# Context attentions: a group's negated maxima are sent to a row of its query tile by eight DMAs, in place of transposes and a subtraction

## The chip, the cores and the metric

The kernel runs on one core of a Trainium2 chip. The metric is the device time of one execution in microseconds (us). The kernel before takes 2529.41 us in the median of three runs (2527.76 to 2529.56). Engines are named as in the profile: PE is TensorE's matrix multiplication and PEld its weight load, DVE is VectorE, ACT is ScalarE, POOL is GpSimd, and SP is SyncE, which here only issues DMAs.

## The reference

The program is a decoder of four layers on x of 4 batches x 256 positions x 128 features, in float32. Each layer has a self attention, a cross attention to one context of 4 x 1601 x 96, and a feed-forward part. Each part is followed by a residual sum and a layer norm. The change concerns the cross attentions of the first and the third layer, called the context attentions here:

```python
x = _layernorm(x + _L0_attn_ref(x, ...))
x = _layernorm(x + _L0_xattn_ref(x, ctx_768, ...))     # context attention, 16 heads of 8
x = _layernorm(x + _L0_ffn_ref(x, ...))
x = _layernorm(x + _L1_attn_ref(x, ...))               # 16 heads of 8, queries and keys normalised
x = _layernorm(x + _L1_xattn_ref(x, ctx_768, ...))
x = _layernorm(x + _L1_ffn_ref(x, ...))
x = _layernorm(x + _L2_attn_ref(x, ...))
x = _layernorm(x + _L2_xattn_ref(x, ctx_768, ...))     # context attention, 16 heads of 8
...                                                    # L2 ffn, then L3 attn, xattn, ffn

def _L0_xattn_ref(x, context, context_mask, Wq, Wk, Wv, Wo):
    ...                                  # q: 16 heads x 256 x 8; k, v: 16 heads x 1601 x 8
    scores = jnp.einsum('bhid,bhjd->bhij', q, k) * scale
    attn = jax.nn.softmax(scores, axis=-1)
    out = jnp.einsum('bhij,bhjd->bhid', attn, v)
    out = out.transpose(0, 2, 1, 3).reshape(B, N, DIM)
    return out @ Wo
```

For a softmax whose exponents stay small, the greatest score of every query (over 1601 keys) is taken from its scores before the exponential.

## The kernel before

The program runs in stages, one after the other: a setup, the self attention of L0 (the first layer), a long stage `middle` (64 to 1115 us in the profile), the feed-forward part of L2, the attentions of L3, and the last part. The change lies in `middle`. It holds the context attentions of L0 and L2 and everything between them.

**Groups and parts.** Four heads make a group. Each head has a slot of 32 partitions in a query tile `Q` (128 x 256) and in a key tile `K` (128 x 1601), of which rows 0 to 7 hold the head's features. Row 16 of each slot (`RS`) is the row of the maxima: in `K` it is one, and in `Q` as computed it is zero, so whatever stands in `Q`'s row 16 is added to all the scores of that query. Two layers, four batches, two key tiles and two query tiles for each give 32 groups, numbered 0 to 31 here. A group's 1601 keys are gone through twice, each time in seven parts.

**Two passes.** The first pass, `maxima` (L951-975), multiplies queries by keys (`one<-K,Q`) and reduces each piece to its maximum (L968, into `M`). With the seventh part, a last reduction (L974) puts 128 x 8 maxima (two halves of the queries, four heads) into columns of a zeroed tile `mpad`. One round later, `shift` (L1065) calls `shifted` (L578-586): it transposes the two halves of `mpad` on TensorE by multiplying with the identity. While `self.narrow` holds, `mm` (L416) cuts a product into pieces of 32 columns, so that a transpose is four products; the sixteen matrix instructions that the profile counts for one group are `one<-c,mpad`. DVE then subtracts the result from `Q` (L585), giving the shifted queries `q2`. The second pass, `scores` (L1020), multiplies keys by `q2`, ACT takes the exponential (L1002, `E`), and `sums` (L1028) multiplies by the values (`one<-E,V`). ACT copies the product (L1045, `part`, two buffers) and POOL adds it to the group's sum (L1046, `acc_sb`).

**The loop.** One pass of the loop from L1125 on is a round, `p`. A round issues the maxima of one part and the scores of another, interleaved by pairs of heads (`jp`: the scores take heads 2 and 3 first), then the sums of the part whose scores were made in the round before. The first pass is up to nine parts ahead of the second. The scores of a group may begin two rounds after its shift, which is three rounds after its last maxima: `shifted_at` (L1148).

**What is woven in.** `life(b)` (L1089) is a generator that each round moves one step on, for each batch: it does the output of L0's context attention, L0's feed-forward part, and the layer L1 up to L2's self attention. Its self attentions hand 24 blocks of four heads, `Own`, to the same loop (16 in L1's attention, 8 in `l1_masked`). An own block first gathers its queries and keys with four DMAs from SBUF to SBUF on SP's queue (L1132; `QK<-w` and `w<-w` in the profile), and keeps the transposes (`own_shift`). In L1's attention (`l1_queries`), POOL raises norms to a power in eight pieces `rn` (L1346), one step of the generator each. `l1_xattn` loads a tile `rows` for each batch (L1381), and `life` of the last batch loads four packs of weights for later stages, `up`, `gp`, `down` and `p3_0` (L1110-1111, by `load`, L371). All of these loads go by SP's queue.

**The order.** `manual_schedule(engines=...)` (L1124) keeps PE, DVE and ACT in the order of the source. POOL's and SP's instructions are placed by the scheduler of the framework, which can move them against the source. A DMA signals its end through one of eight completion semaphores, taken in turn; the next DMA that is given the same semaphore waits for the one before it.

Of the kernel before, what the change touches and what calls it, by code (L numbers as in the profile page):

```python
# [17 lines left out]
ALU = mybir.AluOpType  # L18
AX = mybir.AxisListType
# [3 lines left out]
P = 128  # L23
NB = T // P
# [20 lines left out]
SW = 32  # L45
VS = 17
VW = 2 * 16 * VS + 16
RS, RX = 16, 17
# [14 lines left out]
class Own:  # L63
    pad = q2 = None
# [254 lines left out]
class Net:  # L319
# [48 lines left out]
    def misc(self):  # L368
        return self.tile("one", [P, 512], pool=self.ps_one)

    def load(self, name, keep=False, parts=(0,), width=None):  # L371
        src = self.dram[name]
        if keep:
            t = self.tile(name, [P, src.shape[1]], pool=self.const)
        else:
            t = self.tile(f"w{SLOT[name]}", [P, width or src.shape[1]], pool=self.wpool)
        for lo, hi in zip(parts, parts[1:] + (src.shape[1],)):
            self.nc.sync.dma_start(t[:, lo:hi], src[:, lo:hi])
        self.packs[name] = t

    def loaded(self, name):
# [467 lines left out]
    def middle(self):  # L849
# [7 lines left out]
        nc = self.nc  # L857
# [22 lines left out]
        for i in range(3):  # L880
            t = self.tile(f"V{i}", [P, NCH * 4 * VS + 16], bufs=1)
# [5 lines left out]
        for i in range(5):  # L887
            if i:
                t = self.tile(f"QK{i}", [P, 2, T], bufs=1)
            else:  # L890
                t = self.spot["QK"].rearrange("p (k t) -> p k t", t=T)
# [10 lines left out]
        pairs = [(s, b, kt) for s in range(2) for b in range(B) for kt in range(2)]  # L902
        n_groups = 2 * len(pairs)
        n_parts = 7 * n_groups
        ks, qs, ms, q2s, accs, es, outs = {}, {}, {}, {}, {}, {}, {}
        later, fresh = [], {0: set(range(B)), 1: set()}
        left = {(s, b): 4 for s in range(2) for b in range(B)}

# [42 lines left out]
        def maxima(i, p, jp):  # L951
            if p == 0 and jp == 0:
                ms[i] = self.tile("M", [P, NB, 4, 4], bufs=3)
            heads = [(j, self.misc()) for j in range(2 * jp, 2 * jp + 2)]
            at = 0
            for n, lo, hi in PARTS[p]:
                for j, ps in heads:
                    r = slice(SW * j, SW * j + KR)
                    self.mm(
                        ps[:, at : at + hi - lo], qs[i][r, n * P : (n + 1) * P],  # L960
                        ks[i // 2][r, lo:hi],
                    )
                at += hi - lo
            for j, ps in heads:
                at = 0
                for n, lo, hi in PARTS[p]:
                    part = p - 3 * n
                    nc.vector.reduce_max(  # L968
                        out=ms[i][:, n, j, part : part + 1], in_=ps[:, at : at + hi - lo], axis=AX.X
                    )  # L970
                    at += hi - lo
            if p == 6 and jp == 1:
                pad, at = self.next_mpad()
                nc.vector.reduce_max(out=at, in_=ms.pop(i), axis=AX.X)  # L974
                ms[i] = pad

        def own_maxima(u, jp):
            if jp == 0:
# [41 lines left out]
        def scores(m, jp):  # L1020
            if isinstance(m, Own):
                score(m.t[:, 1, :], m.q2, P, range(NB), jp, m, m.scale)
                return
            i, k = divmod(m, 7)
            cs, kp = chunks(k)
            score(ks[i // 2], q2s[i], kp, cs, jp, m, scale)

        def sums(m):  # L1028
            if isinstance(m, Own):
# [29 lines left out]
        def own_ended(u, sb):  # L1059
# [1 line left out]
            out = outs[u.b][:, :, 4 * u.hd * u.g : 4 * u.hd * (u.g + 1)]  # L1061
            self.collected(sb, out.rearrange("p n (j d) -> p n j d", d=u.hd), u.hd)
            u.count[0] -= 1

        def shift(i):  # L1065
            q2s[i] = self.shifted(qs[i], ms.pop(i), bufs=2)

        def own_shift(u):
            u.q2 = self.shifted(u.t[:, 0, :], u.pad, "Q2s", 2)
# [19 lines left out]
        def life(b):  # L1089
            while left[0, b]:  # L1090
                yield
            yield
            yield from self.l0_output(b, outs.pop(b))
            yield from self.l0_ffn(b)
            qk = yield from self.l1_queries(b)
            yield from attend(b, qk, "qa", 4, 8, 1.0)
            yield
            y = self.y(b)
            nc.vector.tensor_add(y, self.x[b], outs.pop(b))
            yield from self.block_end_steps(b, y)  # L1100
            y = yield from self.l1_xattn(b)
            yield from self.block_end_steps(b, y)
            qk = yield from self.l1_masked(b)
            yield from attend(b, qk, "raw", 2, 16, D**-0.5)
            yield
            yield from self.l1_output(b, outs.pop(b))
            yield from self.l2_attn(b)
            fresh[1].add(b)
            if len(fresh[1]) == B:
                for n in ("up", "gp", "down", "p3_0"):  # L1110
                    self.load(n)
            while left[1, b]:
                yield
            yield CUT if b == B - 1 else None
            yield from self.l2_output(b, outs.pop(b))
            self.gates[b] = yield from self.l2_gate(b)

        self.gates = {}
        lives = [life(b) for b in range(B)]
        engines = {nc.tensor.engine, nc.vector.engine, nc.scalar.engine}  # L1120
        self.narrow = True
        to_shift, shifted_at = {}, {}
        at_m, at_s, last, p, prepared = 0, 0, None, 0, 0
        with self.tc.manual_schedule(engines=engines):  # L1124
            while at_s < n_parts or last is not None or later or line or lives:  # L1125
                for u in [u for u in line if free[u.hd]][:1]:
                    line.remove(u)
                    u.t = free[u.hd].pop(0)
                    for j in range(4):
                        o = (4 * u.g + j) * u.hd  # L1130
                        src = u.qk.rearrange("p (k t) -> p k t", t=T)
                        nc.sync.dma_start(  # L1132
                            u.t[SW * j : SW * j + u.hd, :, :], src[o : o + u.hd, :, :]
                        )
                    u.ready = p + 1
                    under_way.append(u)
                    if u.last:
                        self.drop(u.dense)
                m = s = None
                for u in under_way:  # L1140
                    if m is None and u.pad is None and u.ready <= p:
                        m = u
                    if s is None and u.q2 is not None and u.turn <= p:
                        s = u
                if m is None and at_m < n_parts and at_m - at_s <= 9:
                    if at_m % 14 or prepared > at_m // 14:
                        m = at_m
                if s is None and at_s < n_parts and shifted_at.get(at_s // 7, p) + 2 <= p:  # L1148
                    s = at_s
                own_m = isinstance(m, Own)  # L1150
                ctx_m = not own_m and m is not None
                if own_m:
                    own_maxima(m, 0)
                elif ctx_m:
                    maxima(*divmod(m, 7), 0)
                if s is not None:
                    scores(s, 1)
                    scores(s, 0)
                if own_m:
                    own_maxima(m, 1)  # L1160
                elif ctx_m:
                    maxima(*divmod(m, 7), 1)
                if last is not None:
                    sums(last)
                for f, *args in to_shift.pop(p, ()):
                    f(*args)
                if own_m:
                    to_shift.setdefault(p + 1, []).append((own_shift, m))
                    m.turn = p + 3
                elif m is not None:  # L1170
                    for f, *args in other.pop(m, ()):
                        f(*args)
                    at_m += 1
                    if m % 7 == 6:
                        to_shift.setdefault(p + 1, []).append((shift, m // 7))
                        shifted_at[m // 7] = p + 1
                if first and first[0][0] <= at_m:
                    f, *args = first[0][1:]
                    (st, b, _), part = pairs[args[0]], args[-1]
                    if f is keys or b in fresh[st]:  # L1180
                        f(*args)
                        first.pop(0)
                        if f is keys and part == 2:
                            prepared = args[0] + 1
                if isinstance(s, Own):
                    under_way.remove(s)
                    free[s.hd].append(s.t)
                elif s is not None:
                    at_s += 1
                last = s  # L1190
                self.advance(later)
                self.advance(lives)
                p += 1
# [174 lines left out]
    def l1_xattn(self, b):  # L1368
# [9 lines left out]
        nc.vector.tensor_scalar_add(q, ps[:, :T], self.w("p1", "xqb"))  # L1378
        rows = self.tile("rows", [P, NCH, CR], bufs=1)
        at = slice(b * NCH * CR, (b + 1) * NCH * CR)  # L1380
        nc.sync.dma_start(rows.rearrange("p c d -> p (c d)"), self.dram["ctx_rows"][:, at])  # L1381
        ends = [(lo, min(lo + 512, S2)) for lo in range(0, S2, 512)]
        yield
        ps = self.misc()
# [728 lines left out]
```

## Time and profile before

| | |
|---|---|
| median of three runs | 2529.41 us |
| the profiled execution | 2529.01 us |
| its span, first to last instruction | 2526.8 us |
| mean granted TensorE clock | 0.986 |
| stage `middle` | 64 to 1115 us |
| busy in `middle` (1051 us): PE, DVE, ACT, POOL | 1013.0, 754.1, 694.7, 222.3 us |
| DMA share in `middle` | 0.04 of 16 engines |
| L968, reductions of the first pass, DVE | 1024 of 565 ns |
| L1002, exponentials of the second pass, ACT | 992 of 575 ns |
| L1046, sums on POOL | 192 of 730 ns |

The profile's rows have this form: a line of the kernel, an engine, an operation, the tile written and the tiles read (buffer numbers left out), shapes, and the number of instructions. A row of the timeline begins with its start and its length in us; brackets hold the idle time before it and what ended that. The rows for stretches of time hold, after the length, the busy time of each engine with its number of instructions, then the granted clock (1.00 is full speed), the DMA engines' busy share, and GB/s. "SPq" is SP's queue of instructions, where a DMA's row is its issue: smallest, median and largest duration in ns, then first and last start in us.

### The profile page before, as it was taken

The page shows a single profiled execution, that of the slowest core. Times are in us where ns is not written, and L with a number is a line of the kernel's source. Part 1 is how long each engine was busy: PE and PEld are TensorE (multiplying, and loading weights), DVE is VectorE, ACT ScalarE, POOL GpSimd, SP SyncE. Part 2 cuts the span into 40 slices and gives each one's busy share as a digit, 9 for nine tenths or more (in the row PEclk, how much of TensorE's full clock was granted, in tenths as well). Part 3 has the DMA queues.
Part 4 walks back from the last instruction along what each step waited for, and adds up shares of the span by engine and source line. Part 5 has one row for each costly group of instructions (what it writes and reads, how often), then busy time and mean ns, then how long its engine had stood idle before and what let it go on. Part 6 is the DMA issues. An engine that isn't in the chain of part 4 may idle for free.

```text
span 2526.8 us, 88631 instructions
## 1 busy us (share of the span) xinstructions
PE 2413.9 (96%) x38941; PEld 1668.2 (66%) x38941; DVE 1740.3 (69%) x3802; ACT 1566.3 (62%) x3123; POOL 320.4 (13%) x414
## 2 busy tenths in 40 slices
PE   7999999999999999999999999989899999999997
PEld 4565657666666665668877777766566666666665
DVE  6776766757777777745556666657767776877875
ACT  2676666665666666665535555556666676776674
POOL 3113131131311212110011111011000000000000
PEclk9999999999999999999999999999999999999998
DMA  4000000000000012000030000000000000000000
GB/s 132 2 2 2 7 2 17 7 14 10 2 22 3 2 33 81 2 2 1 1 106 13 26 13 12 12 6 2 2 2 2 5 2 2 5 3 2 5 2 4
DMA packets 14929, 36.19 MB, mean 14 GB/s; under 512 B 4040, under 2 KB 7372, under 8 KB 13648
## 3 DMA queue, kind: packets, MB, share of 16 engines
q1 hardware_dynamic: 14544, 30.53, 4.3%
q8 instruction: 306, 5.01, 0.8%
q14 instruction: 79, 0.65, 0.1%
HBM read 23.67 MB, written 0.52 MB: 10 GB/s over the span
## 4 chain that ended last, share of the span: by engine, by line
PE 83%; DVE 9%; ACT 2%; POOL 2%; issue 2%; POOLq 0%; DVEq 0%; ACTq 0%
PE one L421 68%; PE big L421 14%; DVE M L968 3%; PE one L428 2%; POOL rn L1346 1%; DVE St L1954 1%; DVE ln_st L519 1%; DVE mpad L988 0%; DVE w L1920 0%; ACT E L670 0%; DVE rec L2002 0%; ACT St L1961 0%; DVE ln_mv L521 0%; DVE m L1397 0%; DVE x L530 0%
## 5 line engine op out<-in xcount | busy, mean ns | idle before, releaser
L968 DVE TENSOR_REDUCE M<-one 128x1 f32<-128x458 f32 (+3 forms) x1024 | 513.1, 565 | 160.7 <-PE one L421 160.2
L1002 ACT ACTIVATE E<-one 128x512 f32<-128x512 f32 (+1 forms) x992 | 484.5, 575 | 187.4 <-PE one L421 186.6
L421 PE MATMUL one<-K,Q 32*128 32x458 f32 (+3 forms) x2048 | 435.0, 527 | 3.6 <-ACT part L1045 3.2
L421 PE MATMUL one<-Q,K 32*128 32x256 f32 (+1 forms) x3328 | 396.7, 391 | 0.0
L1910 ACT COPY St<-big 128x1024 f32<-128x1024 f32 (+1 forms) x224 | 204.1, 959 | 133.5 <-PE big L421 133.5
L421 PEld LDWEIGHTS one<-Q,K 32*128 32x128 f32 (+1 forms) x3328 | 262.1, 181 | 34.2 <-issue 5.8
L421 PE MATMUL one<-E,V 128*32 128x256 f32 (+1 forms) x3328 | 230.3, 389 | 19.8 <-DVE M L968 18.1
L1954 DVE TENSOR_TENSOR St<-St,Mb 128x1024 f32<-128x1024 f32 (+1 forms) x224 | 245.2, 1140 | 1.8 <-ACT Mb L1948 1.8
L1961 ACT ACTIVATE St<-St 128x1024 f32<-128x1024 f32 (+1 forms) x224 | 215.4, 1014 | 27.3 <-DVE St L1954 27.0
L421 PE MATMUL one<-St,V 128*32 128x256 f32 (+1 forms) x3328 | 223.5, 387 | 7.7 <-ACT xT L510 6.4
L1046 POOL TENSOR_TENSOR acc_sb<-acc_sb,part 128x256 f32<-128x256 f32 x192 | 140.1, 730 | 703.5 <-ACT part L1045 701.5
L421 PEld LDWEIGHTS one<-K,Q 32*128 32x128 f32 x2048 | 176.0, 184 | 80.0 <-issue 26.2
L421 PE MATMUL big<-Q,K 64*128 64x256 f32 (+1 forms) x1664 | 212.6, 390 | 0.0
L525 POOL TENSOR_TENSOR ln_r<-ln_ve,half 128x2 f32<-128x2 f32 x92 | 68.4, 743 | 1092.0 <-DVE ln_ve L523 1086.6
L1920 DVE TENSOR_TENSOR w<-w,St 128x1024 f32<-128x1024 f32 (+1 forms) x160 | 179.2, 1120 | 32.6 <-ACT St L1910 25.0
L631 DVE TENSOR_REDUCE Ms<-one 128x3 f32<-128x384 f32 x256 | 130.2, 550 | 87.7 <-PE one L421 86.6
L421 PEld LDWEIGHTS big<-Q,K 64*128 64x128 f32 (+1 forms) x1664 | 146.6, 182 | 58.8 <-issue 23.9
L421 PEld LDWEIGHTS one<-E,V 128*32 128x32 f32 (+1 forms) x3328 | 87.0, 109 | 146.7 <-DVE M L968 94.0
L421 PE MATMUL one<-xT,w 128*32 128x256 f32 (+2 forms) x1136 | 164.7, 390 | 4.4 <-DVE M L968 2.5
L421 PEld LDWEIGHTS one<-St,V 128*32 128x32 f32 (+1 forms) x3328 | 113.8, 111 | 70.9 <-ACT xT L510 7.4
L670 ACT ACTIVATE E<-one 128x384 f32<-128x384 f32 x256 | 104.9, 496 | 86.0 <-PE one L421 85.9
L421 PEld LDWEIGHTS big<-w,ctx 96*32 96x32 f32 x3328 | 93.6, 110 | 55.9 <-issue 55.0
(315 smaller groups left out, 4013.8 us busy)
## 6 DMA issues: line engine op xcount, KB each, us to landing
QK<-qk SPq DMA_DIRECT2D x256, 16.0 KB
w<-in_p SPq DMA_DIRECT2D x12, 274.0 KB
rows<-in_ctx_rows SPq DMA_DIRECT2D x4, 630.5 KB
ctx<-in_ctx SPq DMA_DIRECT2D x4, 600.4 KB
w<-in_down SPq DMA_DIRECT2D x1, 2112.0 KB
w<-in_up SPq DMA_DIRECT2D x1, 1632.0 KB
w<-in_gp SPq DMA_DIRECT2D x1, 1632.0 KB
w<-in_p SPq DMA_DIRECT2D x4, 384.0 KB
```

Of the source, the lines that this page charges most:

```text
L421: self.nc.tensor.matmul(out[at], lhsT[:, at], rhs, start=start, stop=stop)
L428: self.nc.tensor.transpose(out, in_, self.ident)
L525: nc.gpsimd.tensor_tensor(rstd, ve, self.half[:, :NB], ALU.pow)
L631: nc.vector.reduce_max(out=m[:, j, :], in_=ps[:, : 3 * P].rearrange("p (s c) -> p s c", c=P), axis=AX.X,)
L670: nc.scalar.activation(es[t, j], ps[:, :w], AF.Exp, scale=scale)
L968: nc.vector.reduce_max(out=ms[i][:, n, j, part : part + 1], in_=ps[:, at : at + hi - lo], axis=AX.X)
L1002: nc.scalar.activation(e[:kp, :w], ps[:kp, :w], AF.Exp, scale=scale)
L1046: nc.gpsimd.tensor_add(accs[i], accs[i], part)
L1910: nc.scalar.copy(st[:kp, :, :nc_, :], ps[:kp, :, :nc_, :])
L1920: nc.vector.tensor_max(to, to, sts[u, k][:kp, :, :nc_, :])
L1954: nc.vector.tensor_sub(e, e, top[u][:kp].unsqueeze(2).broadcast_to([kp, 2, nc_, T]))
L1961: nc.scalar.activation(e, e, AF.Exp, scale=HD**-0.5)
```

## The change

The last reduction of a group now writes a small tile `negm` (128 x 2 x 4, three buffers) with the negated maxima. Eight DMAs on SP's queue, one for each half of the queries and each head, each carry one column of 128 numbers, one from each partition, into half of one row 16 of the query tile itself. The transposes, the subtraction and the tiles `q2s` are gone, and the second pass reads `Q`. The scores of a group may begin three rounds after its last maxima, as before (`turn`). Own blocks keep `own_shift`. The loads of `up`, `gp`, `down`, `p3_0` and of `rows` are issued by ACT in place of SP. POOL's and SP's instructions are now kept in the order of the source too.

```diff
-    def load(self, name, keep=False, parts=(0,), width=None):
+    def load(self, name, keep=False, parts=(0,), width=None, queue=None):
...
-            self.nc.sync.dma_start(t[:, lo:hi], src[:, lo:hi])
+            (queue or self.nc.sync).dma_start(t[:, lo:hi], src[:, lo:hi])
...
             if p == 6 and jp == 1:
-                pad, at = self.next_mpad()
-                nc.vector.reduce_max(out=at, in_=ms.pop(i), axis=AX.X)
-                ms[i] = pad
+                neg = self.tile("negm", [P, NB, 4], bufs=3)
+                nc.vector.tensor_reduce(neg, ms.pop(i), AX.X, ALU.max, negate=True)
+                for n in range(NB):
+                    for j in range(4):
+                        at = SW * j + RS
+                        nc.sync.dma_start(
+                            qs[i][at : at + 1, n * P : (n + 1) * P], neg[:, n, j : j + 1]
+                        )
...
-            score(ks[i // 2], q2s[i], kp, cs, jp, m, scale)
+            score(ks[i // 2], qs[i], kp, cs, jp, m, scale)
...
-        def shift(i):
-            q2s[i] = self.shifted(qs[i], ms.pop(i), bufs=2)
...
                 for n in ("up", "gp", "down", "p3_0"):
-                    self.load(n)
+                    self.load(n, queue=nc.scalar)
...
         engines = {nc.tensor.engine, nc.vector.engine, nc.scalar.engine}
+        engines |= {nc.gpsimd.engine, nc.sync.engine}
...
-                if s is None and at_s < n_parts and shifted_at.get(at_s // 7, p) + 2 <= p:
+                if s is None and at_s < n_parts and turn.get(at_s // 7, p + 1) <= p:
...
                     if m % 7 == 6:
-                        to_shift.setdefault(p + 1, []).append((shift, m // 7))
-                        shifted_at[m // 7] = p + 1
+                        turn[m // 7] = p + 3
...
-        nc.sync.dma_start(rows.rearrange("p c d -> p (c d)"), self.dram["ctx_rows"][:, at])
+        nc.scalar.dma_start(rows.rearrange("p c d -> p (c d)"), self.dram["ctx_rows"][:, at])
```

More of the change, by code (lines that the diff above doesn't have):

```diff
@@ L904, in middle @@
         n_parts = 7 * n_groups
-        ks, qs, ms, q2s, accs, es, outs = {}, {}, {}, {}, {}, {}, {}
+        ks, qs, ms, accs, es, outs = {}, {}, {}, {}, {}, {}
         later, fresh = [], {0: set(range(B)), 1: set()}
@@ L1120, in middle @@
         engines = {nc.tensor.engine, nc.vector.engine, nc.scalar.engine}
+        engines |= {nc.gpsimd.engine, nc.sync.engine}
         self.narrow = True
-        to_shift, shifted_at = {}, {}
+        to_shift, turn = {}, {}
         at_m, at_s, last, p, prepared = 0, 0, None, 0, 0
```

## The prediction

> **What bounds the kernel now.** I read the engine rows and the chain on the page first, then the busy time by stretches, the timeline around one group's end, and last the waits and the DMA issue rows.
>
> ```profile
> PE 2413.9 (96%) x38941; PEld 1668.2 (66%) x38941; DVE 1740.3 (69%) x3802; ACT 1566.3 (62%) x3123; POOL 320.4 (13%) x414
> ...
> PE 83%; DVE 9%; ACT 2%; POOL 2%; issue 2%; POOLq 0%; DVEq 0%; ACTq 0%
> ```
>
> TensorE is busy 96% of the span and holds 83% of the chain that ended last. So work taken from it counts, and a new wait of it counts in full. The change sits in the stage `middle`, 64 to 1115 us, where the columns are length, then busy PE, PEld, DVE, ACT, POOL, the granted clock, DMA.
>
> ```profile
> 150.00:250.00 100.00, 94.10 (x1430) 57.88 (x1422) 70.07 (x163) 64.05 (x148) 30.20 (x32) 0.95 0.01 2
> ...
> 750.00:850.00 100.00, 98.98 (x1921) 68.64 (x1924) 72.19 (x178) 67.76 (x156) 16.56 (x23) 1.00 0.02 5
> ```
>
> The undisturbed stretch leaves TensorE 1 us idle in 100. The other shows an exception: 6 us idle, clock 0.95. The timeline says what that is:
>
> ```profile
> 230.52 12.85 POOL L1346 TENSOR_TENSOR rn<-ss,half 128x8 f32<-128x8 f32 x8
> ...
> 235.52 0.59 PEld L421 LDWEIGHTS one<-E,V 128*32 128x32 f32 x16 [0.35 <-DVE M L968]
> ...
> 236.52 0.19 PEld L421 LDWEIGHTS one<-K,Q 32*128 32x128 f32 x2 [0.41 <-DVE M L968]
> ...
> 237.02 0.19 DVE L974 TENSOR_REDUCE mpad<-M 128x8 f32<-128x32 f32 x1
> ...
> 238.38 0.59 PEld L421 LDWEIGHTS one<-E,V 128*32 128x32 f32 x16 [0.35 <-DVE M L968]
> ...
> 239.05 0.56 PEld L421 LDWEIGHTS one<-c,mpad 128*32 128x32 f32 x16
> ...
> 239.81 0.19 PEld L421 LDWEIGHTS one<-K,Q 32*128 32x128 f32 x2 [0.20 <-issue]
> ...
> 239.95 0.42 DVE L585 TENSOR_TENSOR Q<-Q,one 128x256 f32<-128x256 f32 x1
> ...
> 244.09 0.37 ACT L1045 COPY part<-one 128x256 f32<-128x256 f32 x1 [4.25 <-POOL acc_sb L1046]
> ...
> 244.51 1.90 PE L421 MATMUL one<-K,Q 32*128 32x458 f32 x4 [3.23 <-ACT part L1045]
> ```
>
> A round of the loop is 2.9 to 3.6 us (weight loads of K,Q at 236.52 and 239.81). The eight `rn` powers, one per round in the source, were drawn together into one run of 12.85 us; `acc_sb` adds wait behind it, then ACT, then TensorE, which afterwards runs at clock 0.50 for 6.8 us. Two short stretches, in the same columns as above, show that, and a stall of 2.51 us at 638 that left the clock alone:
>
> ```profile
> 243.20:249.90 6.70, 5.39 (x36) 2.35 (x40) 1.17 (x2) 2.18 (x7) 3.03 (x5) 0.50 0.01 2
> 638.30:645.00 6.70, 4.20 (x80) 2.83 (x80) 6.67 (x19) 2.89 (x8) 0.69 (x1) 1.00 0.01 2
> ```
>
> **The change, part by part.** The sum is against the profiled execution: 2529.01 us, span 2526.8 with 2.2 around it, 0.4 below the median of 2529.41. The built order of the instructions shows TensorE, DVE and ACT otherwise unchanged.
>
> 1. *Transposes gone.* Per group, from the weight load of E,V to that of the next K,Q: 239.81 - 238.38 = 1.43 with the shift, 236.52 - 235.52 = 1.00 without; medians over all such rounds 1.438 and 1.001. So 0.437 x 32 groups = **-14.0 us**, on the path.
>
> 2. *Subtraction gone:* 32 x 0.42 = 13.4 us of DVE, which is busy 72% and waits for TensorE in these rounds: 0 (bounds 0 to -2). The negated reduction replaces one of 188 ns: 0.
>
> 3. *GpSimd in source order.* Each `rn` (1.64 us) now alternates with an `acc_sb` add (0.73): 2.4 us in a round of 2.9 or more, so the run and its stall go; every add is at most 1.6 us later, which the two `part` buffers cover. Three of the four runs cost idle TensorE: 3.23 (here), 4.24 (at 359) and 6.08 (at 525), together 13.55, each followed by clock 0.50 (17.0 us of it outside the gaps; 8.5 us if all were TensorE's). I take 60% of that, 5.1, since the round from 244.51 to 248.96 took 4.45 instead of about 3.4. **-18.6** (bounds -13.5 to -22). The fourth run delayed nothing.
>
> 4. *The new way of the maxima.* After L974, SP issues eight transfers of 128 x 1, then the scores start: the first pair of heads needs the seventh and eighth. The scores' place is unchanged, three rounds on. The time from the end of L974 to the scores' first matmul, group by group, is 2.55 us for the first group, 3.65 for the last, 4.30, 5.38, 5.76, 5.76, 5.87, 6.14, 6.15, 6.49, 6.74, 7.17, 7.57 and above for the rest. Each loses the 0.44 of point 1; group 7 (of 0 to 31; 11.77) loses its 5 us stall too, to 6.3.
>
> What must fit there: wake 0.05 (SP rows start 0.03 to 0.06 after their releaser), seven issue pitches, one transfer, 0.05 for TensorE. No row has 4-byte pieces. The nearest rows:
>
> ```profile
> L1132 SPq DMA_DIRECT2D QK<-w x80: 523/624/1099, 268.3 to 894.3; - x80
> L1132 SPq DMA_DIRECT2D w<-w x16: 507/577/647, 462.4 to 891.2; - x16
> L1381 SPq DMA_DIRECT2D rows<-in_ctx_rows x4: 322/328/348, 38.6 to 711.9; - x4
> ```
>
> Issues between two places in SBUF take 0.58 to 0.62, those from HBM 0.33 to 0.43 whatever their pieces (4 to 256). The new ones are SBUF to SBUF: 0.60, plus 0.045 between issues and 0.047 for a second semaphore wait (both seen at L1132, pitch 0.717 with and 0.668 without): pitch 0.69. Landing: 1.95 to 1.97 after the issue starts, by the semaphore events of L1132 and L1817. L = 0.05 + 4.83 + 1.97 + 0.05 = 6.9. Lateness by group: 4.8, 3.7, 3.0, 2.0, 1.6, 1.6, 1.5, 1.2, 0.85, 0.6, 0.6, 0.2 = **+21.7** (without group 27, next point). Bounds: pitch 0.43 as from HBM gives L 5.1 and 6.3; pitch 0.74 with the longer SBUF landings of the trace (3.2) gives L 8.5 and 47.
>
> The Trainium skill speaks against these transfers: "DMA: Bandwidth & Descriptors", Rules for kernel authors, says that a last dimension that isn't contiguous becomes one descriptor per element and is to be rearranged. No run here shows such a transfer. If each of an engine's eight descriptors took what the trace's 512-byte packets take (27 ns), each landing would be 0.2 us later and this sum 2.4 us larger.
>
> 5. *Loads on ACT's queue.* `up`, `gp`, `down`, `p3_0` are now issued back to back after the ACT copy at 986.46. They hold completion semaphores 0 to 3, and SP's fifth to eighth transfer of group 27 wait for the same four. Singly, 1632 KB landed after 6.4 us and 2112 KB after 8.0: 1.1 + 3.3 per 1000 KB, so 6472 KB land at 987 + 22 = 1009, the eighth transfer at 1011, against scores due at 1003.6 (row at 1004.03): **+7.6** (bounds 0 to 9). The eight issues on ACT, 0.33 each, lie in its idle 38%: 0 to +1, taken as 0. The `rows` loads land in 4.1, long before use.
>
> 6. *SP in source order.* A block's own QK copies now queue behind the eight issues. Group 8's reduction ends at 267.07 and own copies were issued at 268.26 for matmuls at 273.53: pushed to 272.6, last landing 276.7, 3.6 late, of which 0.85 is in point 4: **+2.8** (bounds 0 to 4). Elsewhere at least 0.2 us is left.
>
> 7. *The clock.* In `middle`, gaps of 3.23 and up were followed by 0.50, that of 2.51 at 638 was not. Five stalls of 3 us or more arise (groups 27, 0, 31, 28, own), at 5.1 / 3 = 1.7 each: **+8.5** (bounds 0 to 14). The Trainium skill, "TensorE: Matmul & The Clock Gate", Part 1, halves the clock only after an idle window of about 3.4 us; by that the 3.0 stall goes free, and the sum would be 1.7 lower. The 3.23 row decides for me.
>
> Sum: -14.0 - 18.6 + 21.7 + 7.6 + 2.8 + 8.5 = +8.0, so **2537 us**, 0.3% slower.
>
> **Rivals.** A change under 0.2% (5 us) can hardly be told from none.
> - *Cheap issues, faster.* If an SBUF issue with sixteen engines costs what one from HBM does, pitch 0.43: losses 6.3 + 7.6 + 1 + 3.4 = 18.3, 2529.0 - 32.6 + 18.3 = 2515. For it: out<-x, which reads SBUF, issues in 0.375. Against: every SBUF to SBUF row is 0.51 or more. It decides below a pitch of about 0.60.
> - *Cancelling.* Pitch near 0.6: losses about 32, 2529 within 5 us.
> - *Slow small pieces.* L 8.5: losses 47 + 9 + 5 + 14 = 75, 2571. For it: the piece count, eight transfers in flight at once. Against: the queue moves 2 GB/s here.
>
> **How the numbers follow.** 2537 (2534 to 2552) 0.38; cheap issues 0.27; cancelling 0.20; slow pieces 0.15. Faster 0.27, same 0.20, slower 0.53. The bounds of points 4 and 5 set the range, 2513 to 2567: it takes in the cheap case and most of the slow one.
>
> **What the next profile would show.** Point 1: no `one<-c,mpad` beyond the own ones, 1.0 us from E,V to K,Q. Point 3: no `rn x8`, no TensorE wait on `acc_sb`. Point 4: issues of 0.6, TensorE waits of 1 to 5 us for `Q<-negm` in about twelve groups, the early ones and the last four above all. Point 5: one wait of about 8 us near 1000. Point 7: more half-clock stretches. I am wrong downwards if an issue takes 0.45 or less, upwards if the eighth transfer lands 8 us or more after the reduction.

## The result, and the profile after

The changed kernel takes 2535.27 us in the median of 15 runs (2529.44 to 2541.46), the kernel before 2528.77 in 15 runs beside it (2526.46 to 2533.31). The ratio is 1.0025, with a 95% interval of 1.0017 to 1.0033: 0.25% slower, 6.5 us, against a forecast of 0.3% and 8.0 us. The profiled execution took 2533.71 us (span 2531.9), 4.7 us more than the one before.

The page's engine rows and the chain that ended last, of the changed kernel:

```profile
PE 2419.6 (96%) x38429; PEld 1659.7 (66%) x38429; DVE 1730.1 (68%) x3770; ACT 1567.1 (62%) x3123; POOL 320.4 (13%) x414
...
PE 84%; DVE 9%; ACT 2%; issue 2%; DMA 1%; SPq 0%; POOL 0%; POOLq 0%; DVEq 0%; ACTq 0%
```

TensorE executes 512 matrix instructions fewer and is busy 5.7 us longer. POOL, 2% of the chain before, is down to 0%, and DMA has come in with 1%. The same two stretches of time as before (length, PE, PEld, DVE, ACT, POOL, clock, DMA):

```profile
150.00:250.00 100.00, 97.87 (x1560) 61.92 (x1553) 74.02 (x175) 71.12 (x163) 22.27 (x27) 1.00 0.03 2
750.00:850.00 100.00, 98.98 (x1902) 67.87 (x1900) 71.62 (x177) 67.33 (x156) 16.34 (x23) 1.00 0.05 9
```

Where POOL's run of powers stood, TensorE now does 98 us of work in 100 at full clock (94 at 0.95 before). What came in its place is seen in the timeline at three spots: group 0, an own block behind group 8, and group 27.

```profile
64.99 5.06 SPq L978 DMA_DIRECT2D Q<-negm  x8
...
70.90 2.40 PE L421 MATMUL one<-Q,K 32*128 32x256 f32 x12 [3.80 <-DMA Q<-negm]
...
272.74 5.44 SPq L978 DMA_DIRECT2D Q<-negm  x8
278.28 4.19 SPq L1135 DMA_DIRECT2D QK<-w  x6
...
280.48 1.22 PE L421 MATMUL one<-QK 32*128 32x256 f32 x4 [1.81 <-DMA QK<-w]
...
978.33 0.33 ACTq L378 DMA_DIRECT2D w<-in_up  x1
...
979.67 0.64 ACTq L378 DMA_DIRECT2D w<-in_p  x1
980.41 1.09 ACT L1007 ACTIVATE E<-one 128x512 f32<-128x512 f32 x2 [2.00 <-PE one L421]
...
991.00 8.44 SPq L978 DMA_DIRECT2D Q<-negm  x8
...
1000.09 0.67 PE L421 MATMUL one<-Q,K 32*128 32x256 f32 x2 [2.01 <-DMA Q<-negm]
```

SP needs 5.06 us to issue the eight transfers of group 0, and TensorE stands for 3.80. At 272.74 SP is busy with a group's eight, so the own copies start at 278.28 and TensorE waits for them. At 991 the eight need 8.44, behind loads that ACT issued from 978.33 on. Their four issues also hold ACT itself for 2 us: its exponentials start at 980.41 only. The clock was halved after each of these and after two more waits:

```profile
70.30:80.50 10.20, 9.60 (x72) 6.14 (x72) 3.61 (x9) 3.26 (x6) 0.00 (x0) 0.50 0.01 2
281.90:288.70 6.80, 6.80 (x62) 5.07 (x59) 3.48 (x6) 3.09 (x7) 0.72 (x1) 0.50 0.12 22
1002.10:1008.90 6.80, 6.80 (x49) 3.19 (x48) 2.54 (x5) 3.82 (x9) 0.72 (x1) 0.50 0.00 1
1032.80:1036.30 3.50, 3.50 (x34) 1.30 (x33) 1.49 (x3) 1.70 (x4) 0.00 (x0) 0.51 0.02 5
1107.90:1114.80 6.90, 6.90 (x68) 3.58 (x68) 0.43 (x2) 4.40 (x10) 0.72 (x1) 0.51 0.01 2
```

These are the only stretches in `middle` at half clock. They follow group 0, the own block, and groups 27, 28 and 31. TensorE counts as busy in them because its slower products fill the time. That is one reason why its busy time rose although it has less to do. The other is that many of the waits for the transfers don't show as idle time: idle time that ended with `Q<-negm` comes to 6.9 us at three places, and the pairing below finds losses at eleven groups. At group 1, four `one<-K,Q` products run by themselves from 98.35 to 99.39 us, and the first `one<-Q,K` starts at 99.70, after only 0.31 us of idle time.

DVE executes the same 1024 reductions (L968) in the same order in both kernels, so their starts can be paired one by one. The table gives by how much the difference between the two traces changed at each place:

| place | in the forecast, us | in the traces, us |
|---|---|---|
| each group's border without a wait | -0.44 | -0.43 to -0.45 |
| the three runs of `rn` (243, 359, 525 us) | -18.6 | -6.5, -6.8, -8.7: -21.9 |
| group 0 | 4.8 + 1.7 of clock | +7.1 |
| groups 1 to 4 | 6.7 | +1.5, +1.9, +1.9, +1.3: +6.6 |
| groups 7 and 24 | 1.2 | +2.3, +2.1 |
| own block behind group 8 | 3.6 + 1.7 | +5.7 |
| group 27 | 7.6 + 1.7 | +8.4 |
| groups 28, 30, 31 | 7.9 + 3.4 | +3.3, +0.8, +5.1 |
| other groups | 0.2 | +1.7 |

All that was added comes to some 43 us, all that was removed to 14.0 + 21.9. A half-clock stretch of before at 191.9 us is gone as well (-1.6). The setup, which both have, took 1.1 us longer in this execution, and the stages behind `middle` 2.3 less. Of the 8.4 us at group 27, 1.5 come ahead of its scores, behind ACT's four issues.

### The profile page after: what moved, and what is told of

Its sections match the earlier page's. It is cut to its first block, busy times and chain, and to the rows that moved or that the text cites. A ratio compares the mean times of both kernels' runs of the same rounds, so it can differ in the third digit from the quotient of the medians.

```text
span 2531.9 us, 88233 instructions
## 1 busy us (share of the span) xinstructions
PE 2419.6 (96%) x38429; PEld 1659.7 (66%) x38429; DVE 1730.1 (68%) x3770; ACT 1567.1 (62%) x3123; POOL 320.4 (13%) x414
## 4 chain that ended last, share of the span: by engine, by line
PE 84%; DVE 9%; ACT 2%; issue 2%; DMA 1%; SPq 0%; POOL 0%; POOLq 0%; DVEq 0%; ACTq 0%
PE one L421 68%; PE big L421 14%; DVE M L968 3%; PE one L428 2%; DVE mpad L993 1%; DVE St L1956 1%; DVE ln_st L519 1%; DMA Q<-negm 0%; DVE w L1922 0%; ACT E L670 0%; DVE m L1399 0%; DVE rec L2004 0%; ACT St L1963 0%; DVE x L530 0%; DVE ln_mv L521 0%
## 5 line engine op out<-in xcount | busy, mean ns | idle before, releaser
L968 DVE TENSOR_REDUCE M<-one 128x1 f32<-128x458 f32 (+3 forms) x1024 | 514.5, 566 | 182.0 <-PE one L421 181.5
L421 PE MATMUL one<-K,Q 32*128 32x458 f32 (+3 forms) x2048 | 442.0, 531 | 0.4 <-ACT w L1507 0.4
L421 PE MATMUL one<-Q,K 32*128 32x256 f32 (+1 forms) x3328 | 402.7, 396 | 12.0 <-DMA Q<-negm 6.9
L421 PEld LDWEIGHTS one<-K,Q 32*128 32x128 f32 x2048 | 181.2, 186 | 78.9 <-issue 25.8
L421 PE MATMUL one<-QK 32*128 32x256 f32 (+1 forms) x1344 | 122.4, 374 | 11.1 <-ACT E L670 7.4
```

What stands on the lines that cost most here:

```text
L421: self.nc.tensor.matmul(out[at], lhsT[:, at], rhs, start=start, stop=stop)
L968: nc.vector.reduce_max(out=ms[i][:, n, j, part : part + 1], in_=ps[:, at : at + hi - lo], axis=AX.X)
```

## The experiments

The kernel before ran beside every one of them, at 2528.2 to 2528.6 us in the median.

### What the parts are worth

POOL's order alone, in the kernel before:

```diff
+        engines |= {nc.gpsimd.engine}
```

> The kernel before with one part of the change: POOL in the order of the source. Transposes, subtraction and SP's scheduler stay. My theory (point 3): the three stalls behind the runs of eight rn powers go with their half-clock stretches, 18.6 us (13.5 to 22), so 2510 us (2507 to 2515). The drift between the two traces, which falls by 6.5, 6.8 and 8.7 us at the three places, would say 2507. Rival: the runs of rn cost nothing by themselves, since the rounds behind them catch up or since the stalls only show together with the transposes: 2529 us, as before.

Measured: 2508.21 us, ratio 0.9925 (0.9912 to 0.9939), 20 us less than before. POOL's timeline in this kernel:

```profile
228.82 0.73 POOL L1046 TENSOR_TENSOR acc_sb<-acc_sb,part 128x256 f32<-128x256 f32 x1 [8.25 <-ACT part L1045]
229.68 1.65 POOL L1347 TENSOR_TENSOR rn<-ss,half 128x8 f32<-128x8 f32 x1
232.88 0.73 POOL L1046 TENSOR_TENSOR acc_sb<-acc_sb,part 128x256 f32<-128x256 f32 x1 [1.55 <-ACT part L1045]
```

Powers and adds alternate, POOL idles 1.55 us in the round, and no stretch of `middle` runs at half clock. Paired with the trace before, the gain in `middle` falls at the three places (-6.5, -6.8 and -8.7 us) and at the half-clock stretch of before at 191.9 us, which is gone here too (-1.6). This execution, 2502.24 us, is below the median; some 4 us of its difference lie behind `middle`, which has no part in the change. So this part of the change is a gain by itself and doesn't need the transfers.

The other way round, the changed kernel with POOL left to the scheduler:

```diff
-        engines |= {nc.gpsimd.engine, nc.sync.engine}
+        engines |= {nc.sync.engine}
```

> The changed kernel with POOL left to the scheduler again; SP stays in the order of the source. My theory: the rn powers stand together in runs of eight again and the three stalls come back, 18.6 us (to 22): 2554 to 2557 us. Rival: in the changed kernel the adds have room behind the late scores, so that the runs are hidden: 2535 us.

Measured: 2554.02 us, ratio 1.0105 (1.0091 to 1.0119), 18.8 us above the changed kernel. The run is back in POOL's timeline of this kernel, with the adds queued behind it:

```profile
242.67 12.86 POOL L1348 TENSOR_TENSOR rn<-ss,half 128x8 f32<-128x8 f32 x8
255.49 2.33 POOL L1051 TENSOR_TENSOR acc_sb<-acc_sb,part 128x256 f32<-128x256 f32 x3
```

The late scores didn't hide it. And the changed kernel without its eight transfers:

```diff
-                for n in range(NB):
-                    for j in range(4):
-                        at = SW * j + RS
-                        nc.sync.dma_start(
-                            qs[i][at : at + 1, n * P : (n + 1) * P], neg[:, n, j : j + 1]
-                        )
```

> The changed kernel without the eight DMAs of a group; the maxima are computed but not subtracted. My theory: all that the change costs hangs on these DMAs (points 4 to 7), so what is left is the gain of points 1 and 3, 14.0 + 18.6 = 32.6 us (at most 36): 2493 to 2497 us. No wait on negm, and a half clock only where before had one without POOL. Rival: part of the loss comes from the source order of SP or from the loads on ACT's queue; then the time stays above 2505 us.

Measured: 2500.01 us, ratio 0.9893 (0.9880 to 0.9907). So the transfers cost 35 us in the changed kernel, and all else that it does is worth 28 us of gain. Source order of SP shows no cost without them: the wait at 280 us and the one of group 27 are gone from this trace. The time is still 3 us above the upper end of the expectation, and only 8.2 us below the kernel with POOL's order alone, where 14.0 of transposes separate the two.

Paired with that kernel's trace, this one is only 5.1 us ahead at the end of `middle`. The clock takes most of the rest: this trace has 3.4, 6.8 and 3.4 us at half clock at 52, 69 and 615 us, the other none there, and loses 4.1 us at the first two and 1.5 at the third. Another 1.5 us go behind ACT's four issues for the loads, as in the changed kernel, and 0.9 at 331 us, beside one of the loads of `rows`. So loads on ACT's queue aren't free; no run leaves them on SP's. Of the half clock at 52 and 69 us the cause is open; none of the added transfers stand there. It means that of the 7.1 us at group 0 only some 4 are the transfers': the rest is in this trace too.

### Number, queue and lead of the transfers

Four transfers in place of eight, each with one head's 256 maxima in order (the first pass takes every second query as a block):

```diff
+                neg = self.tile("negm", [P, 4, NB], bufs=3)
...
+                for j in (2, 3, 0, 1):
+                    at = SW * j + RS
+                    nc.sync.dma_start(qs[i][at : at + 1, :], neg[:, j, :])
...
-                        ps[:, at : at + hi - lo], qs[i][r, n * P : (n + 1) * P],
+                        ps[:, at : at + hi - lo],
+                        qs[i][r, :].rearrange("r (p n) -> r n p", n=NB)[:, n, :],
```

> The changed kernel with four DMAs for a group in place of eight: the first pass takes every second query as a block, so that a head's 256 maxima go to one row in order, in pieces of 8 bytes; heads 2 and 3 first. My theory (the lateness is issue pitch times number, then one landing): heads 2 and 3 have landed 0.06 + 0.64 + 1.97 = 2.7 us after the reduction, all four after 4.0, against 5.9 and 6.5. That is late for the first group only (0.7 us); group 27 stays behind the loads, up to 8 us with its clock; own copies wait 2.6 us less. 2528.8 - 14 - 22 + 0.7 + 8 + 1 = 2503 us (2500 to 2510). Rival 1: loading every second query as weights is slower (K,Q weight loads above 184 ns on average); 20 ns more would be some 20 us of weight loads, partly hidden: 2510 to 2523. Rival 2: the lateness doesn't follow the number of DMAs: 2530 or more.

Measured: 2502.74 us, ratio 0.9902 (0.9888 to 0.9916). All four have landed 3.9 us after the reduction in most groups, against 6.5 with eight, and TensorE's idle time that ends with `Q<-negm` is 0.2 us in all, against 6.9. Weight loads of every second query took 191 ns in the mean, 185 in the kernel without transfers; paired with that trace, this kernel loses 0.06 us for a group. (There are 2048 of them, so 20 ns more would have been 41 us and not 20.)

The eight split over two queues:

```diff
-                        nc.sync.dma_start(
+                        (nc.scalar if j in (1, 3) else nc.sync).dma_start(
```

> The changed kernel with the transfers of heads 1 and 3 issued by ACT, those of heads 0 and 2 by SP. My theory (the lateness is the pitch of one queue, 0.64 us, times its transfers): all eight have landed 0.06 + 3 x 0.64 + 1.97 = 4.0 us after the reduction in place of 6.5, late for the first group (1.9 us) and the last (0.8) only. Point 4 falls from about 20 us to 3, point 6 from 5.7 to about 1, point 7 by some 5; group 27 stays behind the loads. That is 26 to 27 us less, 2509 us; against it stand 128 issues on ACT, 70 us in its idle 38%, and ACT's wait for the reduction ahead of its next copy: 0 to 1 us for each group. 2509 to 2535 us, 2515 as the likeliest. Rival: the transfers themselves are slow (eight in flight at once, pieces of 4 bytes), so that two queues land no earlier: 2535 us or more.

Measured: 2589.52 us, ratio 1.0234 (1.0220 to 1.0247), far outside. The first half of the theory held: all eight landed 4.5 us after the reduction in most groups, 2 us earlier, with a pitch of 0.64 on SP's queue and 0.69 on ACT's, and the stall of group 0 was gone. ACT's side I had at 0 to 1 us for a group. Its timeline with TensorE's, and its waits in this kernel (us in total, times, longest):

```profile
89.43 3.74 ACTq L978 DMA_DIRECT2D Q<-negm  x4
93.26 0.37 ACT L1050 COPY part<-one 128x256 f32<-128x256 f32 x1 [4.09 <-PE one L421]
...
93.69 1.39 PE L421 MATMUL one<-K,Q 32*128 32x458 f32 x3 [1.18 <-ACT part L1050]
```

```profile
ACT part L1050 <- DMA Q<-negm: 57.7, 17, 4.4
```

ACT has to pass through the four issues, 2.4 us or more, before its copy of the round's sums, and TensorE waits for the copy. The difference to the changed kernel grows by 1 to 5 us in nearly every group and is 56 us at the end. ACT's idle 38% was no room at that place.

One round more between the passes:

```diff
-                        turn[m // 7] = p + 3
+                        turn[m // 7] = p + 4
...
-                if m is None and at_m < n_parts and at_m - at_s <= 9:
+                if m is None and at_m < n_parts and at_m - at_s <= 10:
```

> The changed kernel with a group's scores one round later (four rounds after its last maxima in place of three) and the first pass up to ten parts ahead in place of nine. My theory: a round of 2.9 us or more covers the lateness of all groups but the first (0.8 us left) and 27 (5 of 8 left). Point 4 goes nearly whole (20 us), point 5 by 3, half of the clock's share (5); point 6 stays. The second pass ends a round later: +1 to 2. 2535.3 - 28 + 2 = 2509 us (2505 to 2516). Rival: the lateness is not what the waits cost, since a round that has only one of the two passes arises at each group's border, with PE waiting for DVE there: 2530 us or more.

Measured: 2509.46 us, ratio 0.9927 (0.9914 to 0.9940). The scores' first products come 8 to 17 us after the reduction in all groups but the first and the last, group 0 waits 1.38 us where it had 3.80, and group 27 doesn't wait. The eight transfers still land at 6.5 to 8.4 us. So for most groups it is the lead that was short by a few us; the rival, a loss through rounds with one pass only, didn't come. The number fits better than its terms: group 27's transfers, at 979 us, now stand 20 us behind the loads (issued from 957.8 on) and don't meet them, so this run doesn't say what a round of lead does there. Point 6's wait, which I had said stays, went at 280 us, but one of 1.69 us for `QK<-w` arose at 417, and the clock was halved at 192.9, 418.2 and 964.3 us.

### The loads and the own copies

The four loads seven rounds later:

```diff
+                for _ in range(7):
+                    yield
                 for n in ("up", "gp", "down", "p3_0"):
                     self.load(n, queue=nc.scalar)
```

> The changed kernel with the loads of up, gp, down and p3_0 seven rounds later, that is behind the eight transfers of group 27. My theory (point 5): the wait of group 27 goes, 8.0 us by the drift between the traces (-8.4 to -0.4 there), so 2527 us (2525 to 2529). The loads have landed some 22 us later, about when group 28's reduction ends; later stages need them 100 us on. Rival 1: the same wait moves to group 28: 2533 us or more. Rival 2: the stall at 998 us is SP's order and not the loads: 2535 us.

Measured: 2529.02 us (2521 to 2538), ratio 1.0002 (0.9989 to 1.0014). Paired with the changed kernel's trace, group 27 gains 5.8 us, and 1.5 more go where the loads were issued before; 1.7 come back where ACT issues them now, and 1.0 at group 28. TensorE's wait there is 2.28 us where it was 1.24, as some of the transfers now land beside the loads (after up to 4.3 us):

```profile
1020.38 1.56 PE L421 MATMUL one<-Q,K 32*128 32x256 f32 x11 [2.28 <-DMA Q<-negm]
```

The rest of the difference lies ahead of that, in the setup and in half-clock stretches of other lengths. The point stands, with a part of the first rival in it. The issues' price only moved.

Own blocks' first pass two rounds behind their copies:

```diff
-                    u.ready = p + 1
+                    u.ready = p + 2
```

> The changed kernel with the maxima of an own block two rounds behind its copies in place of one, so that copies queued behind a group's eight transfers have a round more. My theory (point 6): the wait at 278 us and its half clock go, 5.7 us by the drift between the traces (+5.1 to +10.8 there); elsewhere 24 blocks stand a round later, which costs 0 to 2 us. 2530 us (2528 to 2532). Rival: the copies weren't late by SP's queue but by their source or by the DMA engines; then a round more does it as well, but the issues in the trace start as soon as the copies are due. If the step at 278 us is a matter of group 8's own lateness, the time stays at 2535 us.

Measured: 2546.42 us, ratio 1.0070 (1.0055 to 1.0085), 11 us slower than the changed kernel where 5 faster was expected. The wait at 278 us and its half clock did go. But all that follows stands elsewhere, and near 990 us a new loss arises. ACT's and TensorE's timeline there:

```profile
982.57 0.39 ACTq L378 DMA_DIRECT2D w<-in_gp  x1
988.75 0.33 ACTq L378 DMA_DIRECT2D w<-in_down  x1
994.60 0.34 ACTq L378 DMA_DIRECT2D w<-in_p  x1
995.03 2.06 ACT L1007 ACTIVATE E<-one 128x512 f32<-128x512 f32 x4 [12.72 <-DMA Q<-negm]
...
995.68 1.64 PE L421 MATMUL one<-Q,K 32*128 32x256 f32 x5 [8.51 <-ACT E L1007]
```

The loads now mix with the eight transfers in the turn of completion semaphores: `down` got the semaphore that `up` held, and `p3_0` (`w<-in_p` here) one that a small transfer held, which itself took 8.8 us to land beside the loads. ACT stood in its queue for 12.72 us, and TensorE for 8.51. That a load on a compute engine's queue can stop that engine, beyond the 1.5 us that the four cost in the changed kernel, is what I had not priced (0 to 1 us for the four).

### Putting parts together

Four transfers and later loads:

> Four transfers for a group (heads 2 and 3 first, pieces of 8 bytes) together with the loads of up, gp, down and p3_0 seven rounds later. My theory: with four transfers only group 27 was still late, behind the loads, by 1.3 us in the drift against the kernel without the transfers; that goes, or moves to group 28 in part as it did with eight transfers: 2501 us (2500 to 2504), against 2502.7 with the loads in place. Rival: the later loads hit group 28, which has 2 us less before its scores: 2505 us or more.

Measured: 2502.70 us, ratio 0.9907 (0.9891 to 0.9922), the same as with the loads in place: group 27's wait, 1.2 us in the paired traces, was too small to show in the medians.

And then the own blocks' maxima by four transfers too:

```diff
-                    r = slice(SW * j, SW * j + KR)
+                    r = slice(SW * j, SW * j + RS)
...
+                    u.neg[:, j, :], ps.rearrange("p (n c) -> p n c", n=NB), AX.X, ALU.max,
+                    negate=True,
...
+                for j in (2, 3, 0, 1):
+                    at = SW * j + RS
+                    nc.sync.dma_start(u.t[at : at + 1, 0, :], u.neg[:, j, :])
+                u.q2 = u.t[:, 0, :]
```

> As the one before, and the own blocks' maxima go to row 16 by four transfers too (their first pass multiplies rows 0 to 15 only, so that an old row doesn't count); no transposes of maxima are left in the loop. My theory: a group's transposes cost 0.437 us on TensorE, and an own block's are the same sixteen pieces, so 24 x 0.437 = 10.5 us less: 2490 us (2487 to 2496). The scores of an own block come three rounds behind its maxima, 8 us or more, and its four transfers land within 4. Rival 1: the transfers of blocks and groups queue behind each other and behind own copies (SP then issues 224 + 104 of some 0.64 us in 1051 us, but in bursts): waits of 2 us at a few places, 2495 to 2505. Rival 2: own blocks' transposes filled idle TensorE: 2501, no gain.

Measured: 2504.92 us, ratio 0.9911 (0.9898 to 0.9925): rival 1. Paired with the kernel ahead of it, 0.4 us goes at nearly every own block, but 4.3 and 4.0 us come back at two places. SP's timeline at the first of them:

```profile
263.49 5.99 SPq L1141 DMA_DIRECT2D QK<-w  x8
269.86 2.81 SPq L1001 DMA_DIRECT2D QK<-negm  x4
272.77 2.77 SPq L1141 DMA_DIRECT2D QK<-w  x4
```

One block's four transfers stand ahead of the next one's copies, which TensorE needs at 273.5. A round more for those copies, which had failed with eight transfers and the early loads:

```diff
-                    u.ready = p + 1
+                    u.ready = p + 2
```

> The kernel with four transfers for groups and own blocks and with later loads, and with an own block's maxima two rounds behind its copies in place of one. In the run without that, TensorE waited at 273 and 555 us for copies (QK) that SP issued behind the four transfers of another block, with 6.8 us at half clock after each: 4.3 and 4.0 us. My theory: a round more covers both, so the 10 us of the 24 blocks' transposes show: 2504.9 - 8.3 = 2497 us, or 2492 to 2499. Rival 1: blocks that stand a round later come to lie beside each other differently, and new waits of the same kind arise, as in the kernel with eight transfers, where this delay cost 11 us: 2503 us or more. Rival 2: the gain of the transposes was never there and the time stays at 2503 to 2505 us without such waits.

Measured: 2498.99 us (2496.97 to 2502.20), ratio 0.9883 (0.9864 to 0.9902), at the upper end of what was expected. No wait of TensorE for `QK<-w` is left in its trace, but two stretches at half clock stand at 577.7 and 1001.0 us, and paired with the kernel of four transfers and later loads it is only 3.1 us ahead at the end of `middle`, not 10; where the rest goes wasn't followed. It has the lowest median of all the kernels here, 29 us below the kernel before, though its interval overlaps those of the kernels with four transfers, at 2502.7.

## Why the prediction was right

*Point 1* held to the hundredth: -0.43 to -0.45 us at each border that has no wait. Of its 14.0 us the clock can take some back, as the kernel without transfers shows.

*Point 2*, nothing for the subtraction, held: no border shows more than the transposes.

*Point 3* was right in place and kind, and too small: -21.9 us in the traces, 20.1 as a part alone (ratio's interval: 15 to 22). The term that was too small is the clock. Half of the 17.0 us at half clock is 8.5, and of that I took 60%, from one round; the idle time, 13.55, and all of the 8.5 make 22.0, which is what went.

*Point 4*: the pitch is 0.64 where I had 0.69, and a landing 1.95 to 1.98 where I had 1.97, so L is 6.5 in the quickest groups (0, 2, 12, 26 and 31) and not 6.9. The scores also start half a microsecond earlier than I charged, since their first product needs the seventh transfer only. Both make the sum smaller; what makes it larger again are issues of 0.9 to 1.7 us, one in most groups, and landings of 2.1 to 3.8 us, which push L to 7 or 8 (groups 7 and 24: 4.4 us where I had 1.2; group 24 has no long issue, but its last landing took 3.7). The errors cancel, by luck. The cheap rival needed a pitch below 0.60 and is out; the range that it leaned on, 0.33 to 0.43 for issues from HBM, was also read too narrowly: in the setup those of `x` and `ctx` took 0.47 and 0.63. The slow one needed L at 8.5, which only group 27 passed.

The page that spoke against the transfers, the Trainium skill's "DMA: Bandwidth & Descriptors", Rules for kernel authors, asks to avoid one descriptor for each element. Here 128 pieces of 4 bytes landed after 1.97 us, like eight of 2 KB (1.95 to 1.97 in the trace before): for transfers this small the price was in the issue, and pieces of 8 bytes gained by halving the number of transfers.

*Point 5* had the right place and size: +8.4 with the clock against 9.3. But 1.5 of that are ACT's four issues, taken as 0, which stand in the kernel without transfers too. They took 0.33 to 0.64 each, and ACT's idle 38% wasn't idle there. The way differs in a part as well. Not four but one transfer waited for its semaphore (a pitch of 4.15 before the eighth); the first seven were issued in time and took 5.2 to 8.1 us to land, against 2.0. They landed from 999.06 on, right behind the last load (998.91).

*Point 6*: +5.7 against 5.3 with its share of point 4 and of the clock. It falls away both without transfers and with four of them.

*Point 7*: the five stretches at half clock are at the five places named, but not for the reason given. I counted stalls of 3 us or more; TensorE's idle time there was 3.80 us at group 0 and 1.24 to 2.19 at the other four. The trace before already held such a case, which I passed over: the clock was halved at 191.9 us after a wait of 1.14. And one stretch at group 0 comes without the transfers too. That all five places came out is luck in part.

So the sum, +8.0, met +6.5 with its terms right to a few microseconds, and with errors of both signs: in the traces about 3 us too little gain in point 3, and some 2.5 too little loss in points 4 to 7. By the run without transfers, the transfers cost 35 us where points 4 to 7 make 40.6, and the rest gains 28 where points 1 and 3 make 32.6: both some 5 us too much, which cancels as well.

## What to carry to other kernels

When small DMAs replace engine work, price them as issue pitch times their number plus one landing, and set that against the lead of each consumer, group by group; here halving the number won back 33 of the 35 us, and one round more of lead 26. A queue kept in source order makes everything behind such a burst late, and an engine with idle time on the average has none at the place where it must pass through issues or a semaphore's turn: the four loads cost 1.5 us on ACT, and four transfers for each group 54. Look at each part of a change for itself: here one part, the order of POOL, was worth 20 us and hid what the rest lost.

## What the runs showed of the hardware that was not expected

Some issues on SP's queue take 0.94 to 1.7 us where the median is 0.55: 23 of the 256, spread over the whole of `middle`, in 22 of the 32 groups.

Whether a stall halves the clock depends on more than its length. A stall of 2.5 us, at 638 us in the kernel before, stands at the same instructions in several kernels. In the kernel with POOL's order alone the clock stayed at 1.00, as before:

```profile
613.30:616.80 3.50, 2.73 (x35) 1.32 (x24) 3.36 (x12) 2.68 (x6) 0.48 (x1) 1.00 0.00 0
616.80:620.20 3.40, 1.67 (x24) 0.81 (x28) 3.40 (x9) 0.56 (x2) 0.22 (x1) 1.00 0.00 0
```

In the kernel without transfers it was halved for 3.4 us:

```profile
612.00:615.40 3.40, 1.16 (x18) 0.60 (x10) 3.30 (x12) 2.06 (x4) 0.70 (x1) 1.00 0.00 0
615.40:618.90 3.50, 3.21 (x24) 1.19 (x28) 3.07 (x8) 0.00 (x0) 0.00 (x0) 0.51 0.00 0
```

The stretches are cut on each trace's own grid of 3.4 us, of which the clock's changes lie whole multiples apart. In the first the stall is split over two cells, in the second it lies mostly in one. The Trainium skill, "TensorE: Matmul & The Clock Gate", Part 1, describes a window of 3.4 us that runs freely, which agrees with that. A limit can't be given: in the changed kernel waits of 1.24 to 2.19 us (groups 28, 27 and 31, and the own block) were followed by half clock too, so stalls well below the 3 us that I had counted from can do it. Nor does TensorE's idle time in the profile settle it: ahead of the half clock at 69 us in the kernel without transfers there is no idle time over 0.5 us within 7 us.
